# Graph layers by counted edges: a window's second 128 edges counted in four nodes' columns, and one store moved

## The chip, the cores and the metric

The kernel runs on one core of a Trainium2 chip. The metric is the device time of one execution in microseconds (us); the time before is the median of three runs. All other numbers come from one execution that the hardware profiler recorded.

## The reference

```python
h = relu(layernorm(x))                       # 2500 nodes x 256, fp32
xs = [h]
for W, b in ((W0, b0), (W1, b1), (W2, b2)):  # three edge convolutions
    m = concat([h[dst], h[src] - h[dst]]) @ W + b   # one row for each of 80000 edges
    s = segment_sum(m, dst, num_segments=2500)
    cnt = segment_sum(ones, dst, num_segments=2500)
    h = relu(s / maximum(cnt, 1)[:, None])
    xs.append(h)
return x + concat(xs) @ Wf + bf
```

The edges come sorted by `dst`. A node has 32 incoming edges on average.

## The kernel before

**Counts instead of edges.** The kernel never forms the 80000 rows. For each group g of 480 target nodes it builds a matrix of counts, `a`: how many edges go from source node (128 partitions by 20 tiles t) to each target node. A layer is then a series of matmuls `z x a`, where `z` holds the nodes' products with the lower half of W; `z` is split into `zh` and `zl`, so there are two matmuls for each tile and half of the features. The groups' matrices are built once, in layer 0, written to `a_dram`, and read again for layers 1 and 2. (Layers are counted from 0 here, as `l` is in the code; the change's "layer 2" is `l == 1`.)

**Windows.** Targets are taken in 398 windows of W = 6 neighbouring nodes. A window's edges are the 256 (CAP) edges from its first one on, in two chunks of 128 (CH = 2). `search` finds where each window starts, `get_edges` fetches the 256 sources and targets for 128 windows at a time by an indirect DMA on POOL. `key_parts`, `key_low` and `key_high` turn them into two keys for each edge: the source's low seven bits (`key_m`), and the source's tile combined with the place of the target in the window (`key_n`). An edge whose target lies outside the window gets a key that matches nothing. The first 112 nodes of all (FEW) are not in windows; they sit in the last 128-row block, and their sums are gathered edge by edge (`gather`, `gather_pairs`) into `sums` and joined in `layer_few`.

**From keys to counts.** Blocks of four windows go through three steps. `compare(b)` (VectorE) makes `one_m`, the one-hot of `key_m` over 128 values, and `one_n`, the one-hot of `key_n` over 20 tiles x 6 nodes = 120 columns (NB), both in bf16 and for both chunks of all four windows. `counts(b)` (PE) multiplies them, one matmul for each chunk:

```python
PEo.matmul(pb[:, w * NB:(w + 1) * NB], one_m[:, w * CH + j, :], one_n[:, w * CH + j, :],
           start=(j == 0), stop=(j == CH - 1))
```

`take_counts(b, a)` (ScalarE) copies the 480 columns of the PSUM bank into `a`. There are four buffers of the one-hots (AHEAD), so `compare(b + 4)` waits for the matmuls of block b.

**The order.** Group 0's twenty blocks are counted in the head, together with the layer norm and the first products of all nodes, in an order written out by hand (`order`, a string of step names; "B" is `compare`, "C" `counts`, "E" `take_counts`, "ka" `key_parts`, "se" `search`, "ge" `get_edges`). From then on `layer(0, g)` is woven with the building of group g + 1: three blocks at a time (TURN), seven turns in a group. Calls by `PEo`, `DVEo`, `ACTo`, `POOLo` and `SPo` keep their order in the program on that engine or queue; calls by the plain `SP` may be moved by the scheduler to where their data are ready.

**Around the end of layer 0.** `gather(0)` issues 56 indirect DMAs on POOL, which add into eight rows of `sums`; `add_sums` folds the eight on VectorE, and `layer_few(0)` on PE reads the result after the last group's matmuls. Then `nodes_split(1, t, ...)` makes layer 1's `z` for twenty tiles, each with one store to `z_dram` on SP in order. The last group's matrix is stored by `store_a(NG - 1, ...)` on the plain SP, after these in the program. `gather_pairs(1)` reads `z_dram` on POOL, two edges at a time, and VectorE adds them up among its updates of `acc` (`final`). `load_a` brings the third group's matrix into the buffer of the first when that is done.

If the number of counted edges isn't 80000, a second kernel (`general`) computes everything anew; with these inputs it is skipped.

Of the kernel before, what the change touches and what calls it, by code (L numbers as in the profile page):

```python
# [8 lines left out]
F32 = mybir.dt.float32  # L9
I32 = mybir.dt.int32  # L10
AF = mybir.ActivationFunctionType
OP = mybir.AluOpType
# [250 lines left out]

F32R = mybir.dt.float32r
BF16 = mybir.dt.bfloat16

# [43 lines left out]
def by_windows(ctx: ExitStack, tc: tile.TileContext, x, src, dst, Ws, bs, Wf, bf, out, missing):  # L312
    nc = tc.nc
    PE, DVE, ACT, POOL, SP = nc.tensor, nc.vector, nc.scalar, nc.gpsimd, nc.sync
    PEo, DVEo, POOLo, ACTo, SPo = (InOrder(tc, e) for e in (PE, DVE, POOL, ACT, SP))
    P = 128
    N, D = x.shape
    E = src.shape[0]
# [6 lines left out]
    W = 6  # L325
    CH = 2
    S = 8
    CAP = CH * P
    FEW = 112
    EDGES = 56  # L330
    SUMS = 8
# [4 lines left out]
    IN_LAST = NW - (WG - 1) * P  # L336
    NONE = NP - 1
    NB = NT * W
    BW = 4
    TURN = 3  # L340
    REP = 2
# [49 lines left out]
    nc_ = const.tile([P, W + 2], F32, name="nc_")  # L391
    deg_b = const.tile([P, WG, W], BF16, name="deg_b")
    lim = const.tile([P, WG], F32, name="lim")

    const.tile([P, 24], F32, name="between")
    z_dram = [dram.tile([NP, D], F32, name=f"z_dram{l}") for l in range(L)]
    who = const.tile([P, EDGES], I32, name="who")
    sums = const.tile([P, SUMS, D], F32, name="sums")
# [61 lines left out]
    POOL.memset(shift[:, P:], 0.0)  # L460
    POOL.memset(brow, 0.0)
    nc_i = pp.tile([P, W + 2], I32, name="nc_i")
    POOL.iota(nc_i, pattern=[[-1, W + 2]], base=1, channel_multiplier=0)
    def load_b(l, queue=SP):
        queue.dma_start(brow[PAD:PAD + 1, l % 2, :], bs[l].rearrange("(o d) -> o d", o=1))

# [46 lines left out]
    dst_e = dst.rearrange("(e o) -> e o", o=1)  # L513
    edges = [None] * WG

    def small_numbers():
        DVEo.tensor_copy(iota_m, im_i[:, :P])
        DVEo.tensor_copy(iota_n.rearrange("p (t c) -> p t c", c=W), im_i.rearrange("p (t c) -> p t c", c=S)[:, :, :W])
        DVEo.tensor_copy(nc_, nc_i)

    def limits():
        DVEo.tensor_copy(lim, lim_i)
        DVEo.tensor_copy(limr, limr_i)
        DVEo.tensor_scalar(unlim, lim, -1.0, 0.5, op0=OP.mult, op1=OP.add)
        DVEo.tensor_scalar(after, row_i[:, 0:1], -1.0, float(2 ** 20), op0=OP.is_ge, op1=OP.mult)
        DVEo.tensor_copy(dst_r[:, :MORE], row_i)
# [33 lines left out]
    def search(i, j):  # L560
        sl = slice(i, j)
        DVEo.tensor_add(base[:, 0, sl], base[:, 0, sl], base[:, 1, sl])
        DVEo.tensor_scalar(start_f[:, sl], row[:, sl], float(R), float(HR + P * R - MORE), op0=OP.mult, op1=OP.add)
        DVEo.scalar_tensor_tensor(start_f[:, sl], base[:, 0, sl], -0.5, start_f[:, sl], op0=OP.mult, op1=OP.add)
        DVEo.tensor_scalar(start_i[:, sl], start_f[:, sl], 0.0, float(E - CAP), op0=OP.max, op1=OP.min)

    def get_edges(i):
        es = pp.tile([P, CAP], I32, name=f"es{i}")
        ed = pp.tile([P, CAP], I32, name=f"ed{i}")
        for t, of in ((ed, dst_e), (es, src_e)):  # L570
            POOLo.indirect_dma_start(
                out=t, out_offset=None, in_=of,
                in_offset=bass.IndirectOffsetOnAxis(ap=start_i[:, i:i + 1], axis=0))
        edges[i] = es, ed
# [4 lines left out]
    def key_parts(i):  # L579
        es, ed = edges[i]  # L580
        lo_i = pw.tile([P, CAP], I32, name="lo_i")
        DVEo.tensor_scalar(lo_i, es, P - 1, None, op0=OP.bitwise_and)
        DVEo.tensor_scalar(away[:, i, :], ed, lim[:, i:i + 1], -1.0, op0=OP.subtract, op1=OP.max)
        parts[i] = [lo_i]

    def few_edges():

        es, ed = edges[WG - 1]
        own = pp.tile([P, EDGES], I32, name="own")
        POOLo.tensor_scalar(who, es[:, :EDGES], -NONE, None, op0=OP.add)  # L590
        POOLo.tensor_scalar(own, away[:, WG - 1, :EDGES], 0.0, None, op0=OP.is_equal)
        POOLo.tensor_tensor(who, who, own, op=OP.mult)
        POOLo.tensor_scalar(who, who, NONE, None, op0=OP.add)

# [5 lines left out]
    def key_high(i):  # L600

        es = edges[i][0]
        hi_i = es if i < WG - 1 else pp.tile([P, CAP], I32, name="hi_i")
        DVEo.tensor_scalar(hi_i, es, ~(P - 1), 4, op0=OP.bitwise_and, op1=OP.logical_shift_right)
        kn = pw.tile([P, CAP], F32, name="kn")
        DVEo.scalar_tensor_tensor(kn, away[:, i, :], float(W), hi_i, op0=OP.min, op1=OP.add)
        parts[i].append(kn)

    def key_turn(i):
# [195 lines left out]
    def compare(b):  # L805
        if b >= len(windows):
            return
        g, s, nb = windows[b]
        w0 = sum(GWS[:g]) + s
        one_m = hot.tile([P, BW * CH, P], BF16, name="one_m", bufs=AHEAD)  # L810
        one_n = hot.tile([P, BW * CH, NB], BF16, name="one_n", bufs=AHEAD)
        k = nb * CH
        for one, iota, keys_, m in ((one_m, iota_m, key_m, P), (one_n, iota_n, key_n, NB)):
            DVEo.tensor_tensor(
                one[:, :k, :].rearrange("p k (m r) -> p k m r", r=REP),
                iota.rearrange("p (m r) -> p m r", r=REP).unsqueeze(1).to_broadcast([P, k, m // REP, REP]),
                keys_[:, w0:w0 + nb, :, :].rearrange("p w j r -> p (w j) r").unsqueeze(2)
                .to_broadcast([P, k, m // REP, REP]), op=OP.is_equal)
        ones_of[b] = one_m, one_n

    counted = {}
# [1 line left out]
    def counts(b):  # L823
        _, s, nb = windows[b]
        one_m, one_n = ones_of.pop(b)
        pb = counted[b] = bank()
        for w in range(nb):
            for j in range(CH):
                PEo.matmul(pb[:, w * NB:(w + 1) * NB], one_m[:, w * CH + j, :], one_n[:, w * CH + j, :],
                           start=(j == 0), stop=(j == CH - 1))  # L830

    def take_counts(b, a):
        _, s, nb = windows[b]
        ACTo.copy(
            a[:, :, s * W:(s + nb) * W].rearrange("p t (w c) -> p t w c", c=W),
            counted.pop(b)[:, :nb * NB].rearrange("p (w t c) -> p t w c", w=nb, c=W))

    def build(g, a):

# [14 lines left out]
            store_a(g, a)  # L854
        yield

    def store_a(g, a):
        for t in range(0, NT, 5):
            SP.dma_start(a_dram[g][:, t:t + 5, :], a[:, t:t + 5, :].bitcast(F32))

    def load_a(g):
        a = new_a(g)
# [35 lines left out]
    def rooms(l):  # L898

        for _ in range(AHEAD):  # L900
            two = room()
            yield two[:, 0, :]
            yield two[:, 1, :]
        for i in range(SUMS):
            yield sums[:, i, :]
        for _ in range(AHEAD):
            yield hot.tile([P, BW * CH, NB], BF16, name="one_n", bufs=AHEAD).rearrange(
                "p k m -> p (k m)")[:, :2 * D].bitcast(F32)

    def gather_pairs(l):  # L910
# [35 lines left out]
    def layer(l, g, a, own, PE=PE, ACT=ACT):  # L946
# [32 lines left out]
    kept = [keep_nodes(0, i, j) for i, j in ((0, 4), (10, 16), (16, NT), (4, 8), (8, 10))]  # L979
    acts = {  # L980
        "lim": limits, "first": find_first, "next": find_next, "pick": find_rows,
        "dstr": lambda: ACTo.copy(dst_r[:, MORE:], dst_i),
        "pk": lambda i: pick_half(i // 10, i % 10), "sg": lambda i: count_half(i // 10, i % 10),
        "se": lambda i: search(*((0, 1), (1, WG))[i]), "ge": get_edges,
# [9 lines left out]
        "warm": keep_warm,  # L994
    }
    order = """
        warm8 lim io first next dstr st0 rs0 sq0 sc0 warm12 N0 pick pk00 sg00 pk01 sg01 st1 T0 pk11 R0 st4 rs1 sq1 pk30 se0
        sg11 sc1 Z0 pk20 N1 st5 sg30 ge0 T1 st6 R1 rs3 F0 sg20 pk21 sq3 st7 pk10 H0 F1 rs4 st3 sq4 sc4 G0 st9
        sc3 L0 sg21 N6 pk31 ka0 kb0 Z1 N5 st8 N7 G1 T6 rs5 sg10 sg31 km0 T5 se1 kt0 R6 H1 st2 F6 sq5 sc5 k10 k20
        rs2 Z6 ge1 L1 T7 B0 R5 R7 Z5 B1 C0 B2 ka1 G6 H6 N9 H5 C1 T9 F7 E0 ge2 kb1 R9 sq2 km1 E1 kt1 C2 B3 k21 Z9  # L1000
# [68 lines left out]
    for l in range(1, L):  # L1069
        groups = list(range(NG))  # L1070
        if l % 2:
            groups.reverse()


        last = [t for t in touched(groups[0]) if t]
        for t, zf in zip([t for t in range(1, NT) if t not in last] + last + [0], rooms(l)):
            nodes_split(l, t, zf)
        if l == 1:

            store_a(NG - 1, tiles[NG - 1])  # L1080
        few = gather_pairs(l)
        next(few)
        if l + 1 < L:
            load_b(l + 1)
            load_wb(l + 1)
            load_wt(l + 1)
        finished = []
        for j, g in enumerate(groups):
            now = [t for t in touched(g) if t not in finished]
            for t in now:  # L1090
                final(l, t)
            finished += now
            rest = add_rest(now) if l == 1 else None
            if j == NG - 1:
                load_wf(l + 1)
            for u, _ in enumerate(layer(l, g, tiles[g], LATE)):
                if u % 4 == 1:
                    next(few, None)
                if rest and u in (1, NT):
                    next(rest, None)  # L1100
            if j == 1 and l + 1 < L:
                DVEo.tensor_sub(ws[l + 1][0], ws[l + 1][0], ws[l + 1][1])
            if j + 2 < NG:
                del tiles[g]
                tiles[groups[j + 2]] = load_a(groups[j + 2])
        run(few)
        add_sums(2)
        layer_few(l)
# [41 lines left out]
```

## Time and profile before

| | |
|---|---|
| median of three runs | 512.57 us (512.41 to 512.95) |
| the profiled execution | 510.9 us, span 509.1 us |
| PE busy | 498.3 us (98%) |
| VectorE busy | 262.4 us (52%) |
| ScalarE busy | 135.9 us (27%) |
| GpSimd (POOL) busy | 250.2 us (49%) |
| granted TensorE clock, mean | 0.999 |
| moved by DMA | 98.72 MB, 194 GB/s |

The span is the time from the first to the last recorded instruction. PE is busy when a matmul is under way by the profile's model of its end; neighbouring matmuls overlap, so their spacing says more than their length. PEld is the loading of weights. In lines of groups, the first number after the bar is busy time and the second the mean length in ns. In timelines each line gives the start, the length, engine, source line (L280 is the helper through which all ordered instructions go), operation, output and input, and how many. A bracket tells how long the engine had been idle and what ended that. SPq is SP's queue of DMA issues.

### The profile page before, as it was taken

How to read it: one execution, taken by the hardware profiler on the slowest of the kernel's cores; microseconds unless marked ns; L12 is line 12 of the kernel's file. 1: busy time of each engine (PE TensorE's matmuls, PEld its weight loads, DVE VectorE, ACT ScalarE, POOL GpSimd, SP SyncE). 2: the span in 40 equal slices, each digit the busy share in tenths (PEclk: the TensorE clock that was granted, in tenths of full speed). 3: DMA queues.
4: the chain of work that ended last, by engine and by line, in shares of the span. 5: the costliest groups of instructions: out<-in, count | busy, mean ns of one | idle time of the engine just before them, and what ended most of it. 6: DMA issues, size and time to landing. Idle time of an engine off the chain costs nothing.

```text
span 509.1 us, 7543 instructions
## 1 busy us (share of the span) xinstructions
PE 498.3 (98%) x2875; PEld 410.4 (81%) x2875; DVE 262.4 (52%) x552; ACT 135.9 (27%) x310; POOL 250.2 (49%) x231
## 2 busy tenths in 40 slices
PE   8999999999999999899999999999999999999996
PEld 4898888778788887788687878788887878787885
DVE  7999988888897810782214240415812231213033
ACT  5676667744634310430000000004300000000010
POOL 3694218888888870007666573610176645451000
PEclk9999999999999999999999999999999999999999
DMA  9327987895959898343399999872335878898023
GB/s 277 95 71 135 227 275 242 281 232 163 324 87 363 124 169 306 112 138 94 114 379 338 300 242 285 82 131 85 123 106 196 354 242 279 236 257 84 1 89 119
DMA packets 41475, 98.72 MB, mean 194 GB/s; under 512 B 4999, under 2 KB 31574, under 8 KB 35798
## 3 DMA queue, kind: packets, MB, share of 16 engines
q1 hardware_dynamic: 22198, 68.78, 36.7%
q0 software_dynamic: 18304, 28.26, 32.5%
q10 hardware_dynamic: 928, 1.11, 0.7%
q8 instruction: 24, 0.39, 0.3%
q14 instruction: 21, 0.17, 0.1%
HBM read 60.63 MB, written 37.50 MB: 193 GB/s over the span
## 4 chain that ended last, share of the span: by engine, by line
PE 67%; POOL 19%; DMA 8%; issue 4%; DVE 1%; ACT 0%; DVEq 0%; POOLq 0%; SPq 0%; ACTq 0%
PE pa L961 34%; POOL sums L280 19%; PE bank L781 10%; PE bank L757 7%; PE pa L966 6%; PE pz L280 6%; DMA sums<-z_dram,who 3%; PE bank L280 2%; DMA wf<-in_L_gnn_Wf_dram 2%; DMA z_dram<-zl 1%; DMA z_dram<-zh 1%; PE pa L280 1%; DMA dst_i<-in_dst_dram 1%; PE turned L280 1%; DVE sums L280 0%
## 5 line engine op out<-in xcount | busy, mean ns | idle before, releaser
L280 POOL DMA_INDIRECT one_m<-z_dram,who x112 | 111.0, 991 | 153.2 <-DVE acc L280 40.5
L961 PE MATMUL pa<-a,zh 128*128 128x480 f32 (+1 forms) x400 | 152.8, 382 | 0.0
L961 PE MATMUL pa<-a,zl 128*128 128x480 f32 (+1 forms) x400 | 151.4, 378 | 0.0
L280 POOL DMA_INDIRECT sums<-z_dram,who x56 | 95.7, 1710 | 23.8 <-issue 16.8
L280 DVE TENSOR_TENSOR sums<-sums,one_m 128x512 f32<-128x512 f32 x52 | 36.0, 692 | 106.1 <-DMA one_m<-z_dram,who 104.2
L961 PEld LDWEIGHTS pa<-a,zl 128*128 128x128 f32 x400 | 75.1, 188 | 11.3
L961 PEld LDWEIGHTS pa<-a,zh 128*128 128x128 f32 x400 | 75.1, 188 | 11.0
L280 PE MATMUL pa<-a,zh 128*128 128x480 f32 (+1 forms) x200 | 81.5, 408 | 0.0
L280 DVE TENSOR_TENSOR one_m<-iota_m,key_m 128x1024 bf16<-128x1024 bf16 x100 | 68.6, 686 | 16.5 <-PE bank L280 14.4
L280 PE MATMUL pa<-a,zl 128*128 128x480 f32 (+1 forms) x200 | 75.7, 379 | 0.0
L969 ACT ACTIVATE hT<-pa 128x960 f32<-128x960 f32 (+1 forms) x10 | 9.7, 966 | 232.5 <-PE pa L966 205.0
L280 ACT CAST a<-bank 128x480 fp32r<-128x480 f32 x100 | 51.0, 564 | 59.1 <-PE bank L280 51.5
L280 DVE TENSOR_TENSOR one_n<-iota_n,key_n 128x960 bf16<-128x960 bf16 x100 | 65.0, 650 | 0.0
L280 DVE SCALAR_TENSOR_TENSOR acc<-bank,share,acc 128x256 f32<-128x256 f32 x60 | 28.7, 483 | 65.6 <-PE bank L781 59.1
L781 PE MATMUL bank<-wf,hT 128*128 128x256 f32 x240 | 54.0, 379 | 1.8 <-issue 1.3
L781 PEld LDWEIGHTS bank<-wf,hT 128*128 128x128 f32 x240 | 45.5, 190 | 11.4 <-issue 5.1
L280 PEld LDWEIGHTS <-one_m 128*128 128x128 bf16 x796 | 43.3, 98 | 8.6 <-issue 3.5
L280 PE MATMUL bank<-one_n,one_m 128*128 128x120 bf16 x796 | 48.9, 216 | 0.0
L280 PEld LDWEIGHTS pa<-a,zh 128*128 128x128 f32 x200 | 37.7, 188 | 8.4 <-issue 3.0
L280 PEld LDWEIGHTS pa<-a,zl 128*128 128x128 f32 x200 | 37.6, 188 | 7.0 <-issue 2.1
L757 PE MATMUL bank<-wb,hT 128*128 128x256 f32 x160 | 34.9, 379 | 0.0
L966 PE MATMUL pa<-hT,wt 128*128 128x480 f32 (+1 forms) x80 | 34.0, 565 | 0.1
(145 smaller groups left out, 413.1 us busy)
## 6 DMA issues: line engine op xcount, KB each, us to landing
a<-a_dram SPq DMA_DIRECT2D x20, 1200.0 KB
a_dram<-a SPq DMA_DIRECT2D x16, 1200.0 KB
a_dram<-a SPq DMA_DIRECT2D x4, 1170.0 KB
a<-a_dram SPq DMA_DIRECT2D x4, 1170.0 KB
out_dram<-acc SPq DMA_DIRECT2D x19, 128.0 KB
z_dram<-one_m SPq DMA_DIRECT2D x16, 128.0 KB
z_dram<-sums SPq DMA_DIRECT2D x16, 128.0 KB
acc<-in_x_dram POOLq DMA_DIRECT2D x4, 512.0 KB
```

The costliest lines, as they stand in the source:

```text
L280: return self.tc.keep_in_program_order(call(*args, **kwargs))
L757: PE.matmul(pz[:, :D], hT[:, c, t * P:(t + 1) * P], ws[l][1][:, c, :], start=(c == 0), stop=(c == DC - 1))
L781: PE.matmul(po[:, :D], hT[:, c, t * P:(t + 1) * P], wfs[l][:, c, :], start=(c == 0), stop=(c == DC - 1))
L961: unit[0] = PE.matmul(pa[:, o, :n], z[:, i, o * P:(o + 1) * P], a[:, i, :n], start=(i == 0 and z is zh), stop=(z is zl and last[o] == (kin ...
L966: unit[0] = PE.matmul(pa[:, o, :n], ws[l][0][:, c, o * P:(o + 1) * P], hT[:, c, c0:c0 + n], start=False, stop=(last[o] == (kind, i, o)))
L969: ACT.activation(hT[:, :, c0:c0 + n], pa[:, :, :n], AF.Relu)
```

## The change

- The columns of `one_n` are put in the order (node, tile) instead of (tile, node). The second chunk's one-hot has only the columns of the last four of the six nodes, 80 (N1) of 120. Its matmul adds into the last 80 columns of the window in PSUM. The comparison for `one_n` becomes two instructions, one for each chunk. `take_counts` reads the bank in the new order.
- Places in a window now count from 1 to 6, with 0 for "before it" (`below`, `iota_n`, `nc_`). In the second chunk an edge to one of the first two nodes, or before them, is set to 0, so that it matches nothing.
- For the last block of windows the list of edges must start at the first edge even near the end of the list. The lists are copied in DRAM to two lists that are 256 entries longer (`longer`; four DMAs on SP at the start of the order, two small memsets), and the last block's gathers read these. `search` has one more clamp for it.
- `store_a` for the last group is issued on the ordered SP, behind the twenty stores of `nodes_split` in layer 1.

```diff
+    SKIP = 2
+    N1 = NT * (W - SKIP)
+    below = const.tile([P, WG], F32, name="below")
-    POOL.iota(nc_i, pattern=[[-1, W + 2]], base=1, channel_multiplier=0)
+    POOL.iota(nc_i, pattern=[[-1, W + 2]], base=0, channel_multiplier=0)
...
+    longer = [dram.tile([E + CAP, 1], I32, name=f"longer{i}") for i in range(2)]
+    rest = pp.tile([1, 2, CAP], I32, name="rest")
+
+    def lengthen():
+        for i, of in enumerate((src, dst)):
+            DVEo.memset(rest[:, i, :], -i)
+            SPo.dma_start(longer[i][0:E, :].rearrange("(p c) o -> p (c o)", p=16),
+                          of.rearrange("(p c) -> p c", p=16))
+            SPo.dma_start(longer[i][E:, :].rearrange("(p c) o -> p (c o)", p=1), rest[:, i, :])
...
-        DVEo.tensor_copy(iota_n.rearrange("p (t c) -> p t c", c=W), im_i.rearrange("p (t c) -> p t c", c=S)[:, :, :W])
+        DVEo.tensor_copy(iota_n.rearrange("p (c t) -> p t c", c=W), im_i.rearrange("p (t c) -> p t c", c=S)[:, :, 1:W + 1])
...
+        DVEo.tensor_scalar(below, lim, -1.0, None, op0=OP.add)
...
-        DVEo.tensor_scalar(start_i[:, sl], start_f[:, sl], 0.0, float(E - CAP), op0=OP.max, op1=OP.min)
+        n = min(j, WG - 1)
+        DVEo.tensor_scalar(start_i[:, i:n], start_f[:, i:n], 0.0, float(E - CAP), op0=OP.max, op1=OP.min)
+        if j == WG:
+            DVEo.tensor_scalar(start_i[:, n:], start_f[:, n:], 0.0, float(E), op0=OP.max, op1=OP.min)
...
-        for t, of in ((ed, dst_e), (es, src_e)):
+        for t, of in ((ed, dst_e), (es, src_e)) if i < WG - 1 else ((ed, longer[1]), (es, longer[0])):
...
-        DVEo.tensor_scalar(away[:, i, :], ed, lim[:, i:i + 1], -1.0, op0=OP.subtract, op1=OP.max)
+        DVEo.tensor_scalar(away[:, i, :], ed, below[:, i:i + 1], 0.0, op0=OP.subtract, op1=OP.max)
+        DVEo.scalar_tensor_tensor(away[:, i, P:], away[:, i, P:], float(SKIP + 1), away[:, i, P:],
+                                  op0=OP.is_ge, op1=OP.mult)
...
-        one_n = hot.tile([P, BW * CH, NB], BF16, name="one_n", bufs=AHEAD)
-        k = nb * CH
-        for one, iota, keys_, m in ((one_m, iota_m, key_m, P), (one_n, iota_n, key_n, NB)):
+        one_n = hot.tile([P, BW, NB + N1], BF16, name="one_n", bufs=AHEAD)
+        for one, iota, keys_ in (
+                (one_m[:, :nb * CH, :], iota_m, key_m[:, w0:w0 + nb, :, :].rearrange("p w j r -> p (w j) r")),
+                (one_n[:, :nb, :NB], iota_n, key_n[:, w0:w0 + nb, 0, :]),
+                (one_n[:, :nb, NB:], iota_n[:, NB - N1:], key_n[:, w0:w0 + nb, 1, :])):
...
-            for j in range(CH):
-                PEo.matmul(pb[:, w * NB:(w + 1) * NB], one_m[:, w * CH + j, :], one_n[:, w * CH + j, :],
-                           start=(j == 0), stop=(j == CH - 1))
+            PEo.matmul(pb[:, w * NB:(w + 1) * NB], one_m[:, w * CH, :], one_n[:, w, :NB], start=True, stop=False)
+            PEo.matmul(pb[:, (w + 1) * NB - N1:(w + 1) * NB], one_m[:, w * CH + 1, :], one_n[:, w, NB:],
+                       start=False, stop=True)
...
-            counted.pop(b)[:, :nb * NB].rearrange("p (w t c) -> p t w c", w=nb, c=W))
+            counted.pop(b)[:, :nb * NB].rearrange("p (w c t) -> p t w c", w=nb, c=W))
...
+        "long": lengthen,
-        warm8 lim io first next dstr ...
+        long warm8 lim io first next dstr ...
...
-            store_a(NG - 1, tiles[NG - 1])
+            store_a(NG - 1, tiles[NG - 1], SPo)
```

More of the change, by code (lines that the diff above doesn't have):

```diff
@@ L393, in by_windows @@
     lim = const.tile([P, WG], F32, name="lim")
-    const.tile([P, 24], F32, name="between")
+    below = const.tile([P, WG], F32, name="below")
+    const.tile([P, 16], F32, name="between")
     z_dram = [dram.tile([NP, D], F32, name=f"z_dram{l}") for l in range(L)]
@@ L590, in few_edges @@
         POOLo.tensor_scalar(who, es[:, :EDGES], -NONE, None, op0=OP.add)
-        POOLo.tensor_scalar(own, away[:, WG - 1, :EDGES], 0.0, None, op0=OP.is_equal)
+        POOLo.tensor_scalar(own, away[:, WG - 1, :EDGES], 1.0, None, op0=OP.is_equal)
         POOLo.tensor_tensor(who, who, own, op=OP.mult)
@@ L605, in key_high @@
         kn = pw.tile([P, CAP], F32, name="kn")
-        DVEo.scalar_tensor_tensor(kn, away[:, i, :], float(W), hi_i, op0=OP.min, op1=OP.add)
+        DVEo.scalar_tensor_tensor(kn, away[:, i, :], float(W + 1), hi_i, op0=OP.min, op1=OP.add)
         parts[i].append(kn)
@@ L810, in compare @@
         one_m = hot.tile([P, BW * CH, P], BF16, name="one_m", bufs=AHEAD)
-        one_n = hot.tile([P, BW * CH, NB], BF16, name="one_n", bufs=AHEAD)
-        k = nb * CH
-        for one, iota, keys_, m in ((one_m, iota_m, key_m, P), (one_n, iota_n, key_n, NB)):
+        one_n = hot.tile([P, BW, NB + N1], BF16, name="one_n", bufs=AHEAD)
[3 more added lines that the diff above has]
+                (one_n[:, :nb, NB:], iota_n[:, NB - N1:], key_n[:, w0:w0 + nb, 1, :])):
+            to = one.rearrange("p k (m r) -> p k m r", r=REP)
             DVEo.tensor_tensor(
[L815 to L818, printed above, removed]
+                to, iota.rearrange("p (m r) -> p m r", r=REP).unsqueeze(1).to_broadcast(list(to.shape)),
+                keys_.unsqueeze(2).to_broadcast(list(to.shape)), op=OP.is_equal)
         ones_of[b] = one_m, one_n
@@ L855, in finish, with store_a @@
         yield
-    def store_a(g, a):
+    def store_a(g, a, queue=SP):
         for t in range(0, NT, 5):
-            SP.dma_start(a_dram[g][:, t:t + 5, :], a[:, t:t + 5, :].bitcast(F32))
+            queue.dma_start(a_dram[g][:, t:t + 5, :], a[:, t:t + 5, :].bitcast(F32))
     def load_a(g):
@@ L906, in rooms @@
         for _ in range(AHEAD):
-            yield hot.tile([P, BW * CH, NB], BF16, name="one_n", bufs=AHEAD).rearrange(
+            yield hot.tile([P, BW, NB + N1], BF16, name="one_n", bufs=AHEAD).rearrange(
                 "p k m -> p (k m)")[:, :2 * D].bitcast(F32)
@@ L996, in by_windows @@
     order = """
-        warm8 lim io first next dstr st0 rs0 sq0 sc0 warm12 N0 pick pk00 sg00 pk01 sg01 st1 T0 pk11 R0 st4 rs1 sq1 pk30 se0
+        long warm8 lim io first next dstr st0 rs0 sq0 sc0 warm12 N0 pick pk00 sg00 pk01 sg01 st1 T0 pk11 R0 st4 rs1 sq1 pk30 se0
         sg11 sc1 Z0 pk20 N1 st5 sg30 ge0 T1 st6 R1 rs3 F0 sg20 pk21 sq3 st7 pk10 H0 F1 rs4 st3 sq4 sc4 G0 st9
```

## Prediction

> **What bounds the kernel now.** I read the page's busy shares first, then the chain that ended last, then the busy time in five stretches of layer 0 (the call `layer(0, g)` for g = 0 to 4; l counts from 0).
>
> ```profile
> PE 498.3 (98%) x2875; PEld 410.4 (81%) x2875; DVE 262.4 (52%) x552; ACT 135.9 (27%) x310; POOL 250.2 (49%) x231
> ...
> PE 67%; POOL 19%; DMA 8%; issue 4%; DVE 1%; ACT 0%; DVEq 0%; POOLq 0%; SPq 0%; ACTq 0%
> ```
>
> ```profile
> 60.30:89.70 29.40, 29.40 (x257) 24.57 (x257) 25.04 (x47) 20.34 (x57) 12.17 (x10) 1.00 0.83 268
> 89.70:118.00 28.30, 28.30 (x248) 22.33 (x247) 24.36 (x44) 16.30 (x40) 24.34 (x14) 1.00 0.82 231
> ```
>
> The stretches (length, then the busy time of PE, PEld, DVE, ACT and POOL) show PE never out of work, and its granted clock is 1.00. The chain leaves PE in one place only, for POOL's 56 gathers into `sums`. VectorE is close behind: 24.4 of 28.3 us in the second stretch. So a nanosecond off a matmul counts, as long as VectorE, which makes the matmuls' operands, doesn't take over.
>
> Next I read three rows of the timeline, all bf16 matmuls with new 128x128 weights each time.
>
> ```profile
> 87.43 0.84 PE L280 MATMUL bank<-ident_b,deg_b 128*128 128x64 bf16 x12
> 102.84 1.43 PE L280 MATMUL bank<-one_n,one_m 128*128 128x120 bf16 x24
> 139.22 0.30 PE L280 MATMUL bank<-ident_b,deg_b 128*128 128x14 bf16 x6
> ```
>
> A row's length is (n-1) pitches and one duration, and the durations by shape are 247, 216 and 174 ns. The pitches are (840-247)/11 = 54 ns at 64 columns, (1430-216)/23 = 52.8 ns at 120, and (300-174)/5 = 25 ns at 14.
>
> Last, the end of layer 0, from the timeline and from the chain:
>
> ```profile
> 181.96 2.40 SPq L859 DMA_DIRECT2D a_dram<-a  x4
> ...
> 205.59 0.47 PE L280 MATMUL pa<-only,sums 128*128 128x112 f32 x2 [1.75 <-DVE sums L280]
> ```
>
> ```profile
> 187.23 15.51 DMA sums<-z_dram,who
> 203.12 1.24 DVE sums L280
> ```
>
> The last group's store, 4 x 1170 KB, is issued at 182 us. The last gather is issued at 187.2 and lands at 202.7, 15.5 us on; DMA moves 372 to 379 GB/s from 188 to 200. VectorE needs 2.4 us to fold the eight sums, and PE waits 1.75 us in `layer_few(0)`.
>
> **The change, part by part.**
>
> *Second-half matmuls, 120 to 80 columns.* 398 windows have one such matmul each: 80 in the head, 318 in layer 0. Whether a column is worth 1/2.4 ns depends on what sets the 52.8 ns. The 14-column row has full 128x128 weights at 25 ns, so the weight load isn't the floor. The 64-column row's 54 ns speaks against, but its output is written with a step of six floats and 14 columns of the same kind take 25 ns, so I read it as two cycles a column. One rule speaks against this change: the Trainium skill, "TensorE: Matmul & The Clock Gate", Back-to-back issue gap, says that in a stream of weight loads and matmuls both set the spacing, and gives about 81 ns at 128 columns. By it fewer columns save nothing. The trace has 52.8 ns at 120 and 25 at 14, so I take the row: 40 columns by 0.417 ns = 16.7 ns, or 5.3 us in layer 0 and 1.3 us in the head. Bounds: 0 and 6.6 us.
>
> *Two comparisons for one.* `one_n` of 960 elements lasts 650 ns, and the trace holds a half block of 480 at 402 ns. That makes 0.517 ns an element and 154 ns fixed; 320 elements: 319 ns. Neighbours start 80 ns before the one ahead ends (570 ns from start to start for 960). So the pair takes 322+239 = 561 ns for 570: no change. The skill, "VectorE: DVE Perf Modes", The TRN2 errata, says that each instruction pays its fixed latency, some 150 cycles by its measurement: two would cost 156 ns more less 83 ns for 160 elements, or 73 ns a block. The starts in this trace overlap, so I take 0 and keep +73 ns. In layer 0 it is covered: VectorE waited for PE's banks there for 14.4 us in all. A group takes VectorE 20x1.175 us plus 0.54 for degrees and 1.22 for `by_count`, 25.3 us, against PE's 29.7 (hT to hT), then 28.4. In the head +73 ns would cost up to 24x0.073 = 1.8 us.
>
> *Key arithmetic in the head.* Each `key_parts` gets a second operation over 128x128. The nearest row is `kn`, 420 ns for 256 elements; the same 154 ns and one element a cycle give 287, about 0.28 us with the wait for `away`. Four of them and one more clamp in `search` (about 0.12): 1.2 us. VectorE runs without a gap from 41 to 60 us, and PE's pieces in the chain follow with little room: 16 count matmuls that need 0.84 us took 0.94 at 46.81, because block 12's operand had just ended at 47.10. Step by step: before VectorE's 0.55 us wait for the last edges (at 35.4) it gains 0.9 us of work, and POOL's gather of those edges moves by about 0.4 with its own inputs; so 0.4 us late there, 0.63 at block 12. PE's count of block 12 ends 0.56 late, and the seven blocks after it save 0.067 each, with one more short stall at block 16: about +0.3 us at the head's end, instead of the 1.3 gained. Bounds: -1.3 and +2 us.
>
> *Cheap edits.* The two memsets (0.45 us by the row of 256 elements) and `below` lie before VectorE's 0.85 us wait for dst_i, after a 0.18 us wait for POOL: covered, else 0.5 us. The four DMAs that lengthen the lists are the last ordered ones of SP's first batch, behind wt (issued till 6.8 us); SP then has only the biases until 20.9, and these are needed at 32.5. Their 1.28 MB of reads and writes are some 4 us at the 350 GB/s around them, and DMA is idle from 16 to 20 us. No row shows a copy inside DRAM. It shares the engines with the first edge gather (issued 11.4 to 13.9, used at 17.3). Taken: 0; if it lands late, VectorE stalls by up to 1 us. The last block's gather reads the copies at 31 us, long after. ScalarE now reads a bank at a step of 20 floats; no row has that. Between the same time (480 in 564 ns) and twice that I take the same; twice would be covered in layer 0 (three blocks, 3 us, per turn of 3.7) and might cost 1 to 2 us in the head, where there are two banks.
>
> *The moved store.* It leaves 182 us and goes behind the 20 `z_dram` stores on SP; it passes none of POOL's queue; behind it on SP are layer 2's bias and weights (wanted 100 us later) and `load_a`, which needs its buffer anyway and was issued at 251.7. Without it a gather lands some 1.8 us after its issue (the pair issued by 233.9 was there at 235.8): sums ready at 188.8+0.3+1.8+2.4 = 193.3. PE arrives at 203.7-5.3+0.3 = 198.7. The 1.75 us wait goes, with 5.4 us to spare; had the store stayed, its wait would grow as PE gets faster. At its new place it takes 15 to 16 us (about 219 to 235 then), against layer 1's `gather_pairs` on POOL's queue. VectorE adds those pairs in order with the `acc` updates, and PE waits for these when four banks are full. The row for it: between 252 and 270 us, under the loads of `a`, VectorE waited 10.24 us for a gather, and PE lost nothing. After layer 1's first group PE needs three banks of four. Taken: 0; bound: 0 and +2.5 us.
>
> **Sum.** -5.3 (layer 0) -1.8 (the wait) +0.3 (head) = -6.8; I leave 0.3 for turns in which VectorE is late: -6.5 us. The profiled execution has 510.9 us (span 509.1 and 1.8 around it), so 504.4; it lies 1.7 below the median of 512.57, and the median would be 506.0.
>
> **Rivals.**
> *Columns don't count* (the weight load or the rule above sets the pitch; for: the 64-column row; against: the 14-column row). Only the wait is saved, and the head pays its 0.6: 511.4.
> *Contention*: the moved store holds back layer 1's gathers until `acc` is late, PE stalls for banks, or VectorE is late in more turns. For: the 15.5 us landing; against: no PE loss at 252 to 270. It takes 1 to 4.5 us of the gain: 507 to 510, say 509.
> *Slower: the split comparison loses its paired rate*, by its new steps (200 elements a row, every other key). 800 elements at 1/0.96 ns and 2x72 ns fixed: 0.98 us for 0.57. VectorE then needs 31.6+1.8 = 33.4 us a group against 29.7, +14.8 us over 76 blocks; the head +9.8+0.9; less 1.8: about 536. It passes PE from 0.73 us a pair, and cancels the whole gain at 0.75. Against it: the innermost pair is kept in all three operands, as now.
> *It does nothing*, because the store was never on the path and PE's pitch is unchanged: 512.6.
>
> **How the numbers follow.** A measurement of this kernel can tell about 0.2% (1 us) from no change. Forecast 0.66 (504 to 508.1), columns 0.10 (510.8 to 512.2, about a half beyond 0.2%), contention 0.11, slower 0.10, nothing 0.03. Faster: 0.66+0.11+0.04 = 0.81; same 0.08; slower 0.11. The low end takes in a head that gains its 1.3 us (-8.4: 504.2) and a little of the 1.3 us for which PE idles near 250 us; the high end takes in contention and half of the columns case: 503.7 to 511.2.
>
> **What would show it.** Second-half count matmuls at about 36 ns pitch, so 24 in about 1.24 us for 1.43; groups of layer 0 at 28.4 us for 29.7; `one_n` at 402 and 319 ns; layer 0's `sums` ready before PE, with no wait at `pa<-only,sums`; the store of `a` after the last `z_dram` store; the head's end 0 to 0.5 us later. Wrong if groups stay at 29.7, if VectorE no longer waits for banks in layer 0, or if PE waits at the `acc` products of layer 1.

## The result and the profile after

| | before | after |
|---|---|---|
| median, same chip | 512.49 us (509.81 to 512.95, four executions) | 504.77 us (504.65 to 504.91, four executions) |
| the profiled execution | 510.9 us, span 509.1 | 504.73 us, span 503.0 |
| first matmul of layer 0 | 61.03 us | 61.76 us |
| last `hT` of layer 0's counted groups | 203.26 us | 199.06 us |
| last `acc` | 504.33 us | 496.02 us |

The ratio is 0.986, with a 95% interval of 0.9826 to 0.9894. Ratios in this document leave out executions more than 1.5% above the fastest of the same kernel; medians take in all. The change saves 7.7 us by the medians and 6.1 us between the two spans; the prediction was 506.0 us, 6.5 less than before.

The page of the changed kernel, busy times and shares of the chain:

```profile
PE 492.4 (98%) x2875; PEld 404.6 (80%) x2875; DVE 261.6 (52%) x660; ACT 135.2 (27%) x310; POOL 249.1 (50%) x231
PE 93%; DVE 4%; ACT 1%; POOL 1%; issue 0%; DVEq 0%; ACTq 0%
```

PE is busy for 5.9 us less with the same number of matmuls. The chain now runs along PE nearly everywhere. Before, it left PE for POOL's gathers (19%) and for transfers (DMA 8% in all, of which the last gather's landing is 3%), since PE waited for `sums` at the end of layer 0. That wait is gone, so the chain no longer goes there.

The changed kernel's groups of instructions, forms kept apart (busy us, mean ns, idle before):

```profile
L282 PE MATMUL bank<-one_n,one_m 128*128 128x120 bf16 x398 | 41.0, 218 | 0.5 <-DVE one_n L282 0.5
L282 DVE TENSOR_TENSOR one_n<-iota_n,key_n 128x480 bf16<-128x480 bf16 x99 | 39.9, 403 | 0.0
...
L282 PE MATMUL bank<-one_n,one_m 128*128 128x80 bf16 x398 | 39.8, 199 | 0.0
...
L282 DVE TENSOR_TENSOR one_n<-iota_n,key_n 128x320 bf16<-128x320 bf16 x99 | 31.9, 322 | 0.0
```

Half of the matmuls have 80 columns, and one of each block's two comparisons has 320 elements. The two comparisons last 403 and 322 ns (forecast 402 and 319). The pitch of the pair is 555 ns in the timeline, for 570 before.

Three of the changed kernel's groups of layer 0 (from `hT` to `hT`) in the view of windows: length, busy PE, PEld, DVE, ACT and POOL, granted clock, DMA share, GB/s.

```profile
91.91:121.10 29.19, 29.19 (x261) 23.57 (x262) 25.84 (x68) 16.40 (x41) 25.53 (x13) 1.00 0.81 225
121.10:149.79 28.69, 28.69 (x256) 23.05 (x256) 25.27 (x66) 16.20 (x41) 24.43 (x15) 1.00 0.86 237
149.79:178.03 28.24, 28.24 (x245) 22.72 (x245) 21.54 (x57) 11.29 (x22) 23.67 (x16) 1.00 0.81 225
```

The same three groups before:

```profile
92.49:122.90 30.41, 30.41 (x261) 24.81 (x261) 26.37 (x47) 16.49 (x40) 26.15 (x15) 1.00 0.81 221
122.90:152.82 29.92, 29.92 (x256) 24.28 (x256) 25.61 (x46) 16.38 (x41) 25.35 (x16) 1.00 0.85 230
152.82:182.24 29.42, 29.42 (x245) 23.86 (x245) 21.62 (x40) 11.38 (x22) 25.15 (x15) 1.00 0.94 221
```

Each is shorter by about 1.2 us. PE is still busy throughout, and VectorE, with 21.5 to 25.8 us of work, is still behind it.

The end of layer 0 and the store in the changed kernel's timeline (start, length):

```profile
98.23 1.23 PE L282 MATMUL bank<-one_n,one_m 128*128 128x120 bf16 x24
...
186.97 1.54 POOL L282 DMA_INDIRECT sums<-z_dram,who  x1 [0.30 <-issue]
...
195.93 2.41 DVE L282 TENSOR_TENSOR sums<-sums 128x1024 f32<-128x1024 f32 x3 [15.51 <-DMA sums<-z_dram,who]
...
199.47 0.43 PE L282 MATMUL pa<-only,sums 128*128 128x112 f32 x2
...
219.55 2.87 SPq L282 DMA_DIRECT2D a_dram<-a  x4
```

The first line names a run of 24 count matmuls by its first form: 1.23 us, for 1.43 before. `pa<-only,sums` has no bracket any more: PE didn't wait. But `sums` is ready only at 195.93 + 2.41 = 198.3 us, 1.1 us before PE comes. The store goes out at 219.55, behind the stores of `z_dram`.

### The profile page after: what moved, and what is told of

The parts are those of the page before. It is cut to its first block, busy times and chain, and to the rows that moved or that the text cites. A ratio compares the mean times of both kernels' runs of the same rounds, so it can differ in the third digit from the quotient of the medians.

```text
span 503.0 us, 7659 instructions
## 1 busy us (share of the span) xinstructions
PE 492.4 (98%) x2875; PEld 404.6 (80%) x2875; DVE 261.6 (52%) x660; ACT 135.2 (27%) x310; POOL 249.1 (50%) x231
## 4 chain that ended last, share of the span: by engine, by line
PE 93%; DVE 4%; ACT 1%; POOL 1%; issue 0%; DVEq 0%; ACTq 0%
PE pa L985 34%; PE pa L282 22%; PE bank L804 10%; PE bank L282 9%; PE bank L780 7%; PE pa L990 6%; PE pz L282 4%; DVE one_m L282 1%; DVE one_n L282 1%; POOL acc L282 1%; DVE zl L282 0%; DVE st L282 0%; PE turned L282 0%; DVE away L282 0%; ACT hT L282 0%
## 5 line engine op out<-in xcount | busy, mean ns | idle before, releaser
L282 POOL DMA_INDIRECT sums<-z_dram,who x56 | 94.4, 1686 | 24.0 <-issue 16.8
L282 DVE TENSOR_TENSOR one_m<-iota_m,key_m 128x1024 bf16<-128x1024 bf16 x100 | 68.8, 688 | 13.4 <-PE bank L282 12.4
L282 DVE TENSOR_TENSOR one_n<-iota_n,key_n 128x480 bf16<-128x480 bf16 x200 | 64.1, 362 | 0.0
L282 PEld LDWEIGHTS <-one_m 128*128 128x128 bf16 x796 | 37.4, 98 | 9.5 <-issue 3.5
L282 PE MATMUL bank<-one_n,one_m 128*128 128x120 bf16 (+1 forms) x796 | 42.5, 208 | 0.5 <-DVE one_n L282 0.5
```

The source lines that it names most:

```text
L282: return self.tc.keep_in_program_order(call(*args, **kwargs))
```

## The experiments

The question was which part of the change gave what, and whether each did so for the forecast reason. All ratios are to the kernel before on the same chip.

**1. The store alone.** Before, with one edit:

```diff
-            store_a(NG - 1, tiles[NG - 1])
+            store_a(NG - 1, tiles[NG - 1], SPo)
```

> The kernel before with only the last group's store moved behind layer 1's nodes; counting is unchanged. Theory (the store held back the last gather of layer 0): the wait of 1.75 us before pa<-only,sums goes, so 1.8 to 2.0 us less than before, about 510.6. If moving the store also removes the idle time of 1.25 us near 250 us, which is absent from the profile after, about 509.3. Rival (the gather was late for another reason, or the store only moves the contention to layer 1): within 0.5 us of before.

509.19 us; ratio 0.9906 (0.9872 to 0.994). Its timeline at the end of layer 0:

```profile
187.60 1.54 POOL L280 DMA_INDIRECT sums<-z_dram,who  x1 [0.30 <-issue]
...
195.52 2.41 DVE L280 TENSOR_TENSOR sums<-sums 128x1024 f32<-128x1024 f32 x3 [10.26 <-DMA sums<-z_dram,who]
...
204.05 0.43 PE L280 MATMUL pa<-only,sums 128*128 128x112 f32 x2
```

The gathers land 7.2 us earlier than before (195.5 for 202.7), and the bracket at `pa<-only,sums` is gone. The first 112 nodes' `hT` follows the last group's by 1.77 us for 3.73: the wait is worth 1.96 us. The spans differ by 2.3 us. The ratio says more (3 to 6.6 us), and not all of that is the wait: this profile also lacks a gap that before's chain of waits has near 250 us:

```profile
249.72 0.44 issue
...
250.76 0.81 issue
```

"Issue" is time in which PE waited for nothing that the profile shows. More of this kind comes below.

**2. The counting alone**, run on two chips. The changed kernel, with the store where it was:

```diff
-            store_a(NG - 1, tiles[NG - 1], SPo)
+            store_a(NG - 1, tiles[NG - 1])
```

> The changed kernel with the last group's store back on the free queue, where it is issued as soon as its matrix is ready. Theory: PE reaches layer_few(0) some 4.2 us earlier than before; the store starts as much earlier (near 178 us) and the gather, issued at 187, lands with its end at about 199, so that the sums are ready near 201 and PE waits about 2 us: 506.5 to 507. If the gather's landing stays where it was (202.7), the wait is 6 us: 510.5. Rival (the store is of no account with the faster counting): 504.8.

> e2 once more: the faster counting with the last group's store back on the free queue. In e2 PE had lost 7 us before it came to the end of layer 0, so the gather was there first. Theory: in an execution without these stops the store starts near 178 us, the last gather (issued at 187) lands with the store's end at about 199, and PE waits about 2 us before pa<-only,sums; 506.5 to 507.5 then, 514 to 518 with stops. Rival (the store is of no account): no wait, 504.8 to 506.

517.27 us, ratio 1.0046 (1.0019 to 1.0072), and on the second chip 514.25 us, 1.0049 (1.0021 to 1.0077). So the part that should bring 5 us made the kernel slower. The second run's end of layer 0:

```profile
183.76 2.19 SPq L883 DMA_DIRECT2D a_dram<-a  x4
...
197.53 2.41 DVE L282 TENSOR_TENSOR sums<-sums 128x1024 f32<-128x1024 f32 x3 [11.10 <-DMA sums<-z_dram,who]
```

`sums` is there at 199.9, and PE comes at 205.5. No wait, therefore, and the loss isn't there. It lies in layer 0's first group: from its first matmul to its `hT` it took 38.41 us in the first run and 36.58 in the second, for 30.15 in the changed kernel. PE stood still there again and again, for 4.3 and 3.3 us between 84 and 96 us; the rest of the loss is matmuls that ran slower, at a granted clock down to 0.50. With PE so late, the two runs can't say what the old store costs when counting is faster; that stays open.

**3. All columns.** The changed kernel with `SKIP = 0`: both chunks in 120 columns, everything else kept.

```diff
-    SKIP = 2
+    SKIP = 0
```

> The changed kernel with SKIP = 0: two comparisons, mask, copied lists and moved store as changed, but the second chunk again has all 120 columns. Theory (a column costs PE 0.417 ns, the weights nothing): 398 matmuls x 16.7 ns = 6.6 us come back, of which the head hides some: groups of layer 0 at 29.4 us instead of 28.2, second-half matmuls at 52.8 ns, in all 510 to 512. Rival (the spacing is set by the weight load, and layer 0 got shorter for another reason): 504.8, groups at 28.2 us.

520.62 us; ratio 1.0119 (1.0083 to 1.0155). The groups are back at 30.41, 30.13 and 29.43 us, and the 24 count matmuls at the old length:

```profile
111.66 1.43 PE L282 MATMUL bank<-one_n,one_m 128*128 128x120 bf16 x24
```

So it is the columns that shorten the groups. The head ends at 63.12, 1.36 us later than with 80 columns and 2.1 later than before: that is what the change's additions cost there when no column pays for them. PE stood still between 87.7 and 93 us here too, at the old rate of counting.

**4. Five nodes.** `SKIP = 1`, so 100 columns; one execution.

> The changed kernel with SKIP = 1: the second chunk has 100 columns. Theory (0.417 ns a column): layer 0's groups, from one hT to the next, half way between the changed kernel (29.19, 28.69, 28.24 us) and e3 with 120 columns (30.41, 30.13, 29.43): about 29.8, 29.4, 28.8. Rival (a step somewhere between 120 and 80, as a weight load would make it): equal to one of the two.

516.62 us, with standstills; the two groups behind them took 29.47 and 29.01 us, between those of 120 (30.13, 29.43 in experiment 3) and 80 columns (28.69, 28.24).

```profile
103.47 1.36 PE L282 MATMUL bank<-one_n,one_m 128*128 128x120 bf16 x24
...
130.89:160.36 29.47, 29.47 (x256) 23.86 (x256) 26.21 (x66) 16.32 (x42) 25.20 (x15) 1.00 0.96 229
160.36:189.37 29.01, 29.01 (x245) 23.45 (x245) 22.19 (x57) 11.39 (x22) 22.46 (x14) 1.00 1.07 224
```

So a step that makes 100 columns cost as much as 120 or as 80 is out. But the point is not half way, as expected (29.4 and 28.8): the first 20 columns bring 1.08 us over the two groups (0.86 against before), the next 20 bring 1.55. The 24 count matmuls say the same: 1.36 us, between 1.43 and 1.23. A straight line is not shown, and why it bends stays open. Over all three groups 120 columns take 89.75 us in before and 89.97 in experiment 3, 80 take 86.12: 3.85 us over the 238 second-chunk matmuls in them, or 16.2 ns for 40 columns (15.3 against before). The forecast had 16.7.

**5. Without the added operation.** The changed kernel without the mask in `key_parts`. The mask is a safeguard: without it, an edge to a window's first two nodes in the second chunk would match no column there and yet enter the number of counted edges, so that nothing would notice.

```diff
-        DVEo.scalar_tensor_tensor(away[:, i, P:], away[:, i, P:], float(SKIP + 1), away[:, i, P:],
-                                  op0=OP.is_ge, op1=OP.mult)
```

> The changed kernel without the added operation over the second chunk in key_parts (it leaves out the safeguard that edges to a window's first two nodes in the second chunk are noticed; with these inputs there are none). Theory (VectorE's added key arithmetic sets the head's end, 1.08 us later than before): four times 0.28 us less on VectorE, of which 0.7 to 1.0 us show: about 504.0, layer 0's first matmul at about 61.2 us instead of 61.76. Rival (the head is late because of the copied lists or of POOL): 504.8, first matmul at 61.7.

The head ends at 60.21 us for 61.76, so the mask costs it some 1.5 us. The time from the last `acc` to the end of the span is shorter too: 4.74 us for 6.98. Yet the run took 513.26 us; ratio 0.9961 (0.9937 to 0.9985). Its PE timeline, and its windows in the columns given above:

```profile
83.50 0.23 PE L282 MATMUL bank<-one_n,one_m 128*128 128x120 bf16 x1
84.39 0.37 PE L282 MATMUL bank<-one_n,one_m 128*128 128x80 bf16 x5 [0.66 <-issue]
...
85.84 0.25 PE L282 MATMUL bank<-one_n,one_m 128*128 128x120 bf16 x2 [1.07 <-issue]
86.58 0.21 PE L282 MATMUL bank<-one_n,one_m 128*128 128x120 bf16 x1 [0.49 <-issue]
...
88.72 0.33 PE L282 MATMUL bank<-one_n,one_m 128*128 128x80 bf16 x2 [1.09 <-issue]
```

```profile
84.00:88.00 4.00, 1.18 (x12) 0.58 (x11) 1.92 (x5) 1.12 (x2) 3.22 (x3) 1.00 0.41 122
88.00:92.00 4.00, 2.34 (x14) 1.70 (x15) 2.11 (x9) 1.77 (x6) 3.26 (x3) 0.54 0.46 66
92.00:96.00 4.00, 4.00 (x19) 2.64 (x18) 3.99 (x11) 2.12 (x5) 3.39 (x3) 0.60 0.49 66
```

In the middle of a turn of count matmuls PE stops after one to five of them for 0.5 to 1.1 us, again and again; the brackets name nothing that it waits for. In four microseconds it is busy for 1.18. The granted clock then falls to 0.54 and 0.60, and the matmuls get slower with it: from 92 to 96 us PE is busy throughout with 19 recorded matmuls, where the changed kernel has 38:

```profile
92.00:96.00 4.00, 4.00 (x38) 3.43 (x38) 2.56 (x8) 3.53 (x9) 3.69 (x2) 1.00 0.93 369
```

Such standstills are in the profiles of experiments 2 to 5; the profiles of before, of the changed kernel and of experiment 1 have none here. They cost about what the change brings, so the next runs were for them.

**6. The changed kernel again**, unaltered, on another chip. Theory A: the edits of the experiments have nothing to do with the standstills. Rival: only altered kernels have them.

> The changed kernel, unaltered, beside the next kernel. In the runs of e2, e3 and e4 PE stood still for some 0.7 us at a time, seven to nine times between 83 and 92 us, around its 1250th recorded instruction, with no engine to wait for; the first profile of the changed kernel has none of it. Theory A (these stops depend on the place, on its memory or its neighbours, not on the edits): if this run meets the same chip, it has them too and takes 511 to 513 us. Theory B (they come with the edits of e2 to e4): 504.8 us again, without stops.

Eleven executions from 506.01 to 516.51 us, median 514.57, beside 514.62 for before; ratio 0.9878 (0.9839 to 0.9917). The profiled one, 514.86 us, has the standstills (86 to 92 us), so the rival is out. By the medians the change brought nothing on this chip; the ratio rests on the four shortest of the eleven executions. Three executions took 506.0 to 506.6 us; that these had none isn't seen, since only one was recorded.

**7. The mask later**, on the same chip: moved from `key_parts` to the start of `degrees(i)`, which lies outside the head for most blocks.

```diff
     def degrees(i):
+        DVEo.scalar_tensor_tensor(away[:, i, P:], away[:, i, P:], float(SKIP + 1), away[:, i, P:],
+                                  op0=OP.is_ge, op1=OP.mult)
```

> The changed kernel with the added operation over the second chunk moved out of the hand-ordered head to the start of degrees(i), in layer 0, where VectorE waits for PE 12 us in all. Theory (VectorE's added key arithmetic sets the head's end): the head ends 1 to 1.5 us earlier than in the changed kernel as in e4, and layer 0 hides the operation: 1.0 to 1.5 us less than the changed kernel beside it. Rival (the gain of e4's head is used up by a wait in layer 0): the same time as the changed kernel.

The head ends at 60.54 us for 61.70 in the run before, and the next three groups take 29.18, 28.70 and 28.23 for 29.20, 28.67 and 28.23: in these groups the mask is hidden, and 1.16 us of the head are saved. In the time this is lost among the standstills: 512.89 us, ratio 0.9887 (0.9846 to 0.9928); the fastest execution took 504.73 us for 506.01.

**8. Where the standstills are.** Either a place in PE's stream of instructions (a border between loaded blocks of code, say) or a place in the program. The changed kernel got 2 x 24 one-column matmuls in the warm-up loop (96 records of PE ahead of everything), and the kernel of experiment 7 got 2 x 12.

```diff
+        if cold[0]:
+            for _ in range(24):
+                PEo.matmul(to[:, :1], idle[:, :P], idle[:, :1], start=True, stop=True)
```

> The changed kernel with 48 one-column matmuls more in the head, where PE idles before its first products (they compute nothing that is used): every later instruction of PE stands 96 recorded instructions further back in its stream. PE's stops of 0.7 us in the runs of e2 to e6 lie at recorded PE instructions 1248 to 1332, the last two counting turns of the first group. Theory A (the stops belong to a place in the instruction stream[...]): they stay at 1250 to 1330, which are then 96 instructions earlier in the program, and fall partly on layer matmuls. Theory B (they belong to what the program does there): they move to 1345 to 1430. Without stops 505 us, with them 511 to 516.

> e6 (the added mask moved to layer 0) with 24 one-column matmuls more in the head, so 48 recorded PE instructions further back. Theory A (place in the stream): the slow stretch begins between two counting turns, where PE needs only 9 instructions per us instead of 43, and costs less than in e6: 504 to 509 us, stops still at 1250 to 1330. Theory B (what the program does there): stops at 1296 to 1380, 510 to 514 us as e6.

Count PE's matmuls and weight loads in order of their starts. The standstills came before records 1259 to 1279 in experiment 6; now they come before 1355 to 1371. In experiment 7 they came before 1257 to 1277; with the half dose (48 records) before 1305 to 1325. So they keep their place in the program, the last two counting turns of the first group. A fixed border in the stream is excluded. The Trainium skill, "Runtime: NRT & Kernel Launch", Instruction fetch mechanics, says that instruction buffers are refilled in blocks of 256 instructions, mostly hidden. A block border stays where it is in the stream when 96 records are put ahead; the standstills moved with the program. The times were 508.38 us (0.9889, 0.9846 to 0.9931) and 505.35 us (0.9849, 0.9802 to 0.9896), with before at 514.57.

**9. Without the copies.** Experiment 5's kernel without the lengthened lists; the last windows then miss some edges. One execution.

```diff
-            DVEo.tensor_scalar(start_i[:, n:], start_f[:, n:], 0.0, float(E), op0=OP.max, op1=OP.min)
+            DVEo.tensor_scalar(start_i[:, n:], start_f[:, n:], 0.0, float(E - CAP), op0=OP.max, op1=OP.min)
...
-        long warm8 lim io first next dstr
+        warm8 lim io first next dstr
```

> The changed kernel without the mask (as e4) and without the lengthened lists: the last block reads the lists as before, so the last windows' second chunks miss some edges. Theory (the copies are covered): the head ends as in e4, first layer matmul at 60.2 +- 0.3 us. Rival (the copies delay the first edge gather or the loads of weights): 0.4 us or more earlier than in e4.

509.32 us; the head ends at 59.96 for 60.21. Before and experiment 1 have the same head and end it at 61.03 and 61.42, so 0.25 us is within what such starts differ by. The copies are not shown to cost anything.

**10. Shorter turns.** Experiment 7's kernel with `TURN = 2`: turns of 16 count matmuls rather than 24.

> e6 (mask in layer 0) with two blocks of counts a turn instead of three (TURN = 2), ten turns a group, so that PE's bursts of 43 instructions per us last 0.7 us instead of 1.1. If PE's stops near 84 to 92 us need long bursts, they are rarer: most executions near 504 us, against 510 to 515 for most of e6's. If they belong to the program's place or time and not to bursts: 510 to 514 as e6. Without stops the turns themselves change nothing (PE-bound): 503 to 505; if VectorE is late in the shorter turns, up to 2 us more.

506.34 us (504.52 to 508.52); ratio 0.9878 (0.985 to 0.9907). Two pauses were left in the profile, 0.89 us (a wait for ScalarE's `a`) and 0.62 us with nothing named, on the chip where the counting-alone kernel had a median of 514.25. The groups are 0.25 to 0.65 us longer. Shorter turns may help, or the other order of the program; the run doesn't tell these apart. Its interval, like those of experiments 7 and 8, overlaps the changed kernel's: no version was shown to be faster.

## Why the prediction was right

Between the two recorded executions the steps measure as follows.

| step | forecast, us | measured, us |
|---|---|---|
| layer 0, fewer columns | -5.3, with 0.3 given back | -4.93 (142.23 to 137.30, first matmul to last `hT`) |
| wait before `pa<-only,sums` | -1.8 | -1.96 |
| head | +0.3 | +0.73 |
| standstills near 250 and 386 us | not in the sum | -2.15 |
| from the last `acc` to the end of the span | not in the sum | +2.2 |
| span | -6.5 | -6.1 |

*Columns.* The step that carried the forecast was right: 40 columns are worth 16.2 ns (forecast 16.7), and columns do count, as the 14-column row had said. Half of them brought less than half (experiment 4), so 0.417 ns for each column is right for this step only. The skill's spacing of about 81 ns at 128 columns for such a stream is far off in these traces, which have 52.8 ns at 120 and, where 120 and 80 alternate, 24 in 1.23 us, or (1230-199)/23 = 45 ns each; that rival is out.

*Comparisons.* Two for one cost nothing: 555 ns for 570, so each instruction's fixed part overlaps with its neighbour's. VectorE still waited for banks in layer 0, 12.4 us for 14.4. The slower rival, losing the paired rate, would have shown 0.98 us a pair.

*The head* was under-estimated by 0.4 us, about as much as two starts of the same head differ. Its terms were better than the sum: columns gain 1.36 us there (forecast 1.3), by experiment 3; the mask costs 1.5 and 1.2 by experiments 5 and 7. What failed is the step "0.4 late there, 0.63 at block 12": block 12's operand is 1.1 us later (45.85 to 46.95), so less of the four operations was absorbed than assumed.

*The end.* After the last `acc` the changed kernel needs 6.98 us to the end of its span, for 4.77 before. The prediction had no term for this, nor for the 2.15 us that the missing standstills give; that the two cancel is luck. The profiles divide by the mask: it is 6.9 to 7.2 us in all that have it, wherever it stands, and 4.7 to 4.8 in before and in experiments 1, 5 and 9, which don't. (In 5 and 9 some 0.8 us more lie between the span and the whole time.) Why an operation on VectorE in the head or in layer 0 should lengthen the end was not looked into; the cause is open.

*The wait.* Right in size, but the margin was wrong: 1.1 us and not 5.4. The mis-sized term is "lands some 1.8 us after its issue". Without the store, the last gather lands 9.0 us after its issue begins in the changed kernel (186.97 to 195.93) and 7.9 us in experiment 1 (187.60 to 195.52), for 15.5 in before. From 188 to 196 us the changed kernel moves 67 GB/s, 0.54 MB in 8 us, or four gathers of 131 KB; that makes some 2.0 us each, an estimate that counts all of it as gathers. POOL issues one every 1.84 us, so by this estimate its queue is behind, and the last has others ahead of it. The row taken for 1.8 us was a plain pair in layer 1, with nothing ahead.

*The moved store* holds back layer 1's gathers, as forecast, and PE doesn't notice. The changed kernel's VectorE timeline:

```profile
235.20 0.69 DVE L282 TENSOR_TENSOR sums<-one_m 128x512 f32<-128x512 f32 x1 [10.76 <-DMA a_dram<-a]
...
247.38 0.69 DVE L282 TENSOR_TENSOR sums<-sums,one_m 128x512 f32<-128x512 f32 x1 [5.70 <-DMA one_m<-z_dram,who]
```

and its chain of waits at the same time:

```profile
242.49 2.59 PE bank L804 x12
245.07 17.36 PE pa L985 x80
```

VectorE waits for 10.76 and 5.70 us, and PE goes from one group to the next without a gap. The contention rival is out for this execution.

*ScalarE's stepped read* takes 565 ns for 564, so of its two bounds the lower one held.

*The median.* The profiled execution was to be 504.4 and was 504.7. The median was put 1.7 us above it because before's was; after's are equal, and so the medians differ by 7.7 us where the recorded executions differ by 6.2. Before's executions differ by 3 us here and by more on other chips, and its profile has standstills that after's lacks, which the prediction knew only as "PE idles near 250 us". The 504.77 us also belong to four executions that, by their times, met no long standstills: the same kernel had a median of 514.57 us on another chip. The prediction had no term for them.

What stays open: why PE stands still, why the end is longer with the mask, why, by the times, experiments 2, 3 and 5 met it in all executions and the first four of the changed kernel in none, and whether executions that aren't recorded have the same.

## What to carry to other kernels

If a trace has one kind of matmul in two widths, the difference of their pitches says whether columns are paid for, and one width that runs faster than the supposed floor rules that floor out. Take a transfer's landing time from a row of the same kind with the same queue ahead of it, since an idle queue's row says nothing of a backlog. When one part of a change, run alone, goes the other way, look in the profile for where the time went before doubting the part; here it lay in another place and was in the unaltered kernel too.

## What the runs showed of the hardware

- PE can stand still for 0.4 to 1.2 us at a time between matmuls, with nothing in the profile that it waits for. In the profiles with the long stretch (experiments 2 to 9) it always lay at the same place of the program, in turns of short matmuls with new weights, and made the first group 6 to 9 us longer: 3 to 5 us of standing still, the rest matmuls at a granted clock that fell to 0.50 to 0.60 in stretches of 4 us. Judging by the times it comes and goes from execution to execution, and its share differs from chip to chip.
- Gathers of 128 rows of 1 KB that add into their target take some 2.0 us each by an estimate from the 67 GB/s moved (66 in experiment 1), with no other large transfer. POOL issues one every 1.84 us, and the last lands 8 to 9 us after its issue.
- A bf16 matmul with new 128x128 weights costs 16.2 ns less with 80 columns than with 120, or 0.40 ns a column; 100 columns lie between, nearer to 120. The weight load, 98 ns long in the profile, is no floor: where 120 and 80 columns alternate, the matmuls follow each other at 45 ns.
- Reading PSUM at a step of 20 floats takes ScalarE 565 ns for 480, and 564 in runs of six.
